# Two-operand VectorE operations in a four-layer mixer: the mean feature stays in PSUM, row sums move to GpSimd, the second batch is transposed by DMA, and the order of the work is written anew

## The chip, the cores and the metric

The kernel runs on one core of a Trainium2 chip: TensorE (PE, matmuls), VectorE (DVE), ScalarE (ACT), GpSimd (POOL) and SyncE (SP, which only issues DMAs here). The metric is the device time in microseconds (us) of one execution; a kernel is given by the median of its runs. All data is fp32. [...]

## The reference

Eight batches of 512 rows and 256 features pass through four layers, each added to its input `x` after a layer norm of it.

```python
x = x + attn_a(ln(x))            # Q, K = l2norm(x Wq), l2norm(x Wk); V = x Wv
                                 # Q * mean over rows of (K * V)
x = x + ffn(ln(x))               # "f": r * (relu(xk Wk)^2 Wv), r = sigmoid(xr Wr)
                                 # xr = mu_r x + (1-mu_r) x_prev, xk likewise; x_prev: the row before
x = x + attn_b(ln(x))            # 16 heads of 64: q, k, v with biases,
                                 # softmax over the queries (axis=2), output weights and bias
x = x + ffn(ln(x))               # "g", the same weights as "f"
```

## The kernel before, in words

**Stages and names.** In names, `b` is the batch, `h` one of two halves of 256 rows, `u` one of two blocks of 128 rows in a half. A batch passes through: `linear` and `queries` (layer one's K, V, Q, prefix `a`), `mean` and `front` (the mean feature and its product with Q), `front_ffn` (prefix `f`), `front_norm` (prefix `n`: the norm for the attention), then the attention, `project_out` or `project_out_fast` (tiles `m_y`), and `tail` (the second ffn, prefix `g`). The attention runs over `g` = 8 b + p, pairs of heads: `project_pairs` makes `qk` of two pairs with seven products in place of eight (`seven`, tiles `m_qk`, drained by ACT at L957 and DVE at L901, L911, L921, L965); `values_fast` does the same for `v` (tiles `m_v`). Then for each of four chunks `c` of 128 keys: `scores` (PE, L1258, tile `sc`), the maximum over the queries (DVE, L1263, `nm`), `exps` (ACT, L1274, `e`, with sums), `scale_v` (DVE reciprocal L1287, POOL product L1291, `vs`), `context` (PE, L1311, `cx`), drained at L1318 and L1319. Tiles that end in `True` belong to batch 1, and to the second ffn of batches 0 to 6; those in `False` to the other fronts and to `g7`.

**The order is written out by a planner.** The class `Order` takes generators ("chains") that yield steps: an engine, a cost in us, a time from which it may run. It keeps a clock for each engine and emits the instructions in the order in which it lets the steps run; the program fixes that order for every engine. Two pairs of heads form a period; `attend` writes their attention out, and `until` and `fill` put the other chains between, after due times in `PLAN` and a row of `CHOICES` for each period (a share of time, a slack, a seed for the ranks, and shifts of single chains). The planner also hands out five PSUM places: three of two banks (scores take them first) and two of one (context takes those). An engine runs its instructions strictly in the order written, so a late one holds all behind it.

**Norms.** `normed` takes the mean and variance (DVE, L377, L378, tiles `st`, `mv`); POOL then makes `shift` and `rstd` with two operations with constants (L395, L396; the early form has one, L383), a power (L397, L384) and a product (L398); ACT (L401) or, in the early form, DVE (L387) applies them. The result is turned either by PE (`normed_t`, L415, four transposes of 128 x 128 and a copy out of PSUM) or by a DMA (`normed_dma`: two POOL copies that set 16-bit halves apart, L428; a DMA transpose on SP's queue, L433; a POOL copy back, L437). Before the change batches 0 and 1 take PE at every norm of their front, the later ones the DMA.

**Time mixing.** `mixed_t` (from PSUM, L491, L501) and `mixed_dma` (from SBUF, L526, L532) form `xr` and `xk`; `first_column` fills the first row of a half from the last row of the half before (`edge`, L471).

**The mean feature.** `mean` multiplies a matrix of 1/512 with the products of K and V (L738), ACT copies the PSUM result to `gf` in SBUF (L741) and the bank is free; `front` then has DVE form `q * rn * gf` in four instructions a batch (L753), and adds it to `x` (L627; DVE for batches 0 and 1, and for the last tail, else POOL). `rows_of_output` ends with DVE adding the attention's result to `x` (L1199).

**Loads.** SP's queue issues x0, weights, x1, `aq`, `ak`, `av`, then `al` (written at L1352), x2 and x3. The biases are loaded from POOL's queue by `load_biases` (L331 to L335) within `mean` of batch 0. Batch 0's `v` are plain matmuls (`values`, L1024): eight blocks of two matmuls of 512 columns.

Of the kernel before, what the change touches and what calls it, by code (L numbers as in the profile page):

```python
# [8 lines left out]
F32 = mybir.dt.float32  # L9
# [29 lines left out]
    (3, 0, 38258, (9, 6)), (2, 0, 40677), (1, 0, 35919), (0, 0, 10543), (5, 2, 39456, (56, 6)),  # L39
    (4, 1, 34514), (2, -1, 72430), (6, 0, 70518), (1, 2, 57519), (4, 1, 11881), (0, 0, 0),  # L40
    (2, 0, 49737, (112, 6), (111, -24), (107, -24)), (-4, 1, 2083), (-3, -1, 8923),
    (-1, -1, 78359), (-3, 0, 30936), (-1, 1, 3181), (-1, 0, 25662, (161, 6)), (5, -1, 77260),
    (-2, 0, 42609), (-3, 0, 9127), (-2, 0, 32981), (2, -1, 46208), (-2, 0, 74670),
    (0, 1, 37804, (203, -6)), (3, 0, 36325),
    (3, 2, 41178, (216, 24), (219, -12), (217, 6), (240, 12)), (0, 0, 57144, (247, -24)),
    (5, 2, 47853), (4, 2, 81239), (-2, 2, 86574), (1, 0, 68043), (1, 0, 9189), (-4, 0, 55291),
# [12 lines left out]
    "v 0": (-1, 0), "v 1": (3, 0), "project": (-1, 0), "sums": (0, 0), "late sums": (5, 0),  # L59
# [34 lines left out]
class Order:  # L94
# [5 lines left out]
    def __init__(self):  # L100
        self.free = {"T": 0.0, "A": 0.0, "V": 0.0, "G": 0.0, "S": 0.0}
        self.chains, self.period, self.spent, self.count = [], -1, 0.0, 0
        self.open = -1
        self.marks = {None: 0.0}

        self.banks = [0.0] * (PAIRS + BANKS)
        self.current, self.at = None, 0.0
# [79 lines left out]
    def first(self, a):  # L187
        c = min(a, key=self.start)
        same = [d for d in a if d.on == c.on and self.start(d) <= self.start(c) + 0.4]
        return min(same, key=lambda d: (d.rank > -NP and d not in self.banks, d.rank + self.turn(d)))  # L190
# [5 lines left out]
    def turn(self, c):  # L196

        v, n = self.choice[2], c.number
        moved = sum(by for m, by in self.choice[3:] if m == n)
        if v == 0:  # L200
            return moved
        h = (n * 2654435761 + v * 40503 + v * n % 97 * 7919) & 0xFFFFFFFF
        h = ((h ^ h >> 13) * 1274126177) & 0xFFFFFFFF
        return ((h >> 8) % 1000 / 1000 - 0.5) * (24, 12, 6)[v % 3] + moved
# [49 lines left out]
def kernel(ctx: ExitStack, tc: tile.TileContext, a: dict, out: bass.AP):  # L254
# [73 lines left out]
    dvb = const.tile([P, 2, 2 * P], F32, tag="dvb", name="dvb")  # L328

    def load_biases():  # L330
        nc.gpsimd.dma_start(out=vb, in_=a["vb"].partition_broadcast(P))  # L331
        nc.gpsimd.dma_start(out=bias[:, 0, :], in_=a["qb"])
        nc.gpsimd.dma_start(out=bias[:, 1, :], in_=a["kb"])
        nc.gpsimd.dma_start(out=lb[:, 0, :], in_=a["lb"].partition_broadcast(P))
        nc.gpsimd.dma_start(out=lc, in_=a["lb"].rearrange("(k p) -> p k", p=P))  # L335
        order.place("G", 2.0, 0.0)
# [34 lines left out]
    def normed(src, name, s, h, ready, early=False):  # L371

        ready = yield "V", 1.2, ready
        mv = small.tile([P, 2, 2], F32, tag="mv", name=f"mv_{name}_{h}")
        for u in range(2):
            st = small.tile([P, 6], F32, tag="st", name=f"st_{name}_{h}_{u}")
            nc.vector.bn_stats(st, src[:, 2 * h + u, :])  # L377
            nc.vector.bn_aggr(mv[:, u, :], st)  # L378
        xn, rstd = tiles(s["xn"], h), small.tile([P, 2], F32, tag="rstd", name=f"rstd_{name}_{h}")
        if early:  # L380

            ready = yield "G", 1.05, ready
            nc.gpsimd.tensor_scalar(rstd, mv[:, :, 1], LN_EPS, 1.0, ALU.add, ALU.mult)  # L383
            nc.gpsimd.tensor_tensor(rstd, rstd, neg_half[:, :2], ALU.pow)  # L384
            ready = yield "V", 0.75, ready
            for u in range(2):
                nc.vector.tensor_scalar(  # L387
                    xn[:, u, :], src[:, 2 * h + u, :], mv[:, u, 0:1], rstd[:, u : u + 1],
                    ALU.subtract, ALU.mult,
                )  # L390
        else:

            shift = small.tile([P, 2], F32, tag="shift", name=f"shift_{name}_{h}")
            ready = yield "G", 1.4, ready
            nc.gpsimd.tensor_scalar(shift, mv[:, :, 0], -1.0, None, ALU.mult)  # L395
            nc.gpsimd.tensor_scalar(rstd, mv[:, :, 1], LN_EPS, 1.0, ALU.add, ALU.mult)  # L396
            nc.gpsimd.tensor_tensor(rstd, rstd, neg_half[:, :2], ALU.pow)  # L397
            nc.gpsimd.tensor_tensor(shift, shift, rstd, ALU.mult)  # L398
            ready = yield "A", 1.0, ready
            for u in range(2):  # L400
                nc.scalar.activation(  # L401
                    xn[:, u, :], src[:, 2 * h + u, :], AF.Identity,
                    bias=shift[:, u : u + 1], scale=rstd[:, u : u + 1],
                )
        return ready
# [60 lines left out]
    def first_column(prev, name, h, i):  # L466

        if h == 0:
            nc.vector.memset(prev[:, :, 0:1], 0.0)
        else:  # L470
            nc.vector.tensor_tensor(  # L471
                prev[:, :, 0:1], edge[name], omu[:, i, :].unsqueeze(2), ALU.mult
            )
# [256 lines left out]
    def mean(b, ready):  # L730

        if b == 0:
            nc.gpsimd.tensor_scalar(omu, mu, -1.0, 1.0, ALU.mult, ALU.add)
            order.place("G", 0.2, 0.0)
            load_biases()
        ready = yield "T", 0.43, ready
        ps = bank(f"gf_{b}")
        nc.tensor.matmul(ps[:, :D], lhsT=mean_s, rhs=means[b], start=True, stop=True)  # L738
        ready = yield "A", 0.3, ready
        gf = one.tile([P, D], F32, tag="gf", name=f"gf_{b}")  # L740
        nc.scalar.copy(gf, ps[:, :D])  # L741
        order.give()
        for h in range(2):
            order.add(front(b, h, gf, ready), *due_of("front", b))

    def front(b, h, gf, ready):
# [3 lines left out]
        ready = yield "V", 0.79, ready, -1, ("q", b, h)  # L750
        rn, qs = halves[b, h], tiles(s["r"], h)
        for u in range(2):
            nc.vector.scalar_tensor_tensor(  # L753
                qs[:, u, :], qs[:, u, :], rn[:, u : u + 1], gf, ALU.mult, ALU.mult
            )
# [3 lines left out]
    def front_ffn(b, h, ready):  # L759

        ready = yield from ffn(
            x[b], f"f{b}", buffers(b == 1), h, ready, adder(b), b >= 2, None
# [3 lines left out]
    def front_norm(b, h, ready):  # L766
# [9 lines left out]
        if b < 2:  # L776
# [10 lines left out]
        if not both(f"f{b}"):  # L787
            if b == 0:
                order.add(values(0, 0), "v 0")
                order.add(values(0, 1), "v 1")  # L790
# [183 lines left out]
    def values_fast(b, half):  # L974
# [5 lines left out]
        yield "G", 0.0, 0.0, -1, ("vs", NP * (b - 1) + 3 + 4 * half, 1)  # L980
# [33 lines left out]
    def values(b, half):  # L1014
# [3 lines left out]
        for t in range(NT):  # L1018
# [9 lines left out]
            issued("plain_v", 2 * NT, done)  # L1028
# [148 lines left out]
    def rows_of_output(b, h, ready):  # L1177
# [19 lines left out]
        ready = yield "V", 0.62, ready  # L1197
        xt = half_of(x[b], h)
        nc.vector.tensor_tensor(xt, s["xn"][:, h, :], xt, ALU.add)  # L1199
# [170 lines left out]
    order.add(sums_of_weights(av, "sums_v", split_values, "plain_v"), "late sums")  # L1370
# [88 lines left out]
```

## Time and profile before

| what | value | from |
|---|---|---|
| median of 3 runs | 1143.93 us (1142.75 to 1144.15) | the times |
| the profiled execution's own time | 1144.05 us | its run |
| its span, first to last instruction | 1142.3 us | the page |
| first matmul starts | 6.34 us | timeline |
| last matmul starts | 1136.86 us | trace |
| granted TensorE clock | 1.00 of full speed | view of the cores |
| moved by DMA | 33.10 MB, mean 29 GB/s | the page |
| DVE maximum of the scores (L1263) | 306.9 us in 256 instructions | groups |
| ACT exponentials (L1274) | 346.5 us in 512 instructions | groups |

A page has the busy time of each engine, the span in 40 slices, the DMA queues, the chain of work that ended last, and the costliest groups of instructions. A row of a group reads: line, engine, operation, output<-inputs, shapes, xcount | busy us, mean ns of one | the engine's idle time just before, and what ended most of it. A timeline's row has start, length, engine, line, operation, tiles, shapes, count, and in brackets the idle time before it with its releaser. In this trace an fp32 matmul has two records, a transpose one.

### The profile page before, as it was taken

To read this page: it belongs to the slowest core of one execution; us is meant where nothing else is said; L and a number is where in the kernel's file an instruction comes from. 1 tells how busy PE (TensorE), PEld (TensorE's weight loads), DVE (VectorE), ACT (ScalarE), POOL (GpSimd) and SP (SyncE) were. 2 spreads that over 40 slices of the span, in tenths; PEclk is the share of its full clock that TensorE was granted. 3 is DMA by queue.
4 is the path that set the end of the run, shared out by engine and by line. 5 is a ranking of instruction groups with operands and counts; after the bars stand their busy time and mean duration, and the time that the engine had idled before them with its cause. 6 is when DMAs were issued, how large, how long until landed. Compare 5 with 4: busy or idle time off the path is not lost.

```text
span 1142.3 us, 19417 instructions
## 1 busy us (share of the span) xinstructions
PE 1116.8 (98%) x6942; PEld 698.6 (61%) x6942; DVE 805.7 (71%) x1470; ACT 676.4 (59%) x1785; POOL 568.8 (50%) x883
## 2 busy tenths in 40 slices
PE   7999999999999999999999999999999999999998
PEld 4654556665756667565676656676565765656556
DVE  4877577678577785777857777668776677665755
ACT  4557665377455774556745676457755477554753
POOL 4475224554465544655546555465454754343321
PEclk9999999999999999999999999999999999999999
DMA  8001000110111100122011120121101110001101
GB/s 299 1 1 20 1 1 1 38 28 11 19 38 38 28 11 19 38 38 29 10 29 35 31 29 10 39 37 20 29 19 29 20 38 20 10 11 28 20 1 37
DMA packets 78640, 33.10 MB, mean 29 GB/s; under 512 B 68401, under 2 KB 77105, under 8 KB 78033
## 3 DMA queue, kind: packets, MB, share of 16 engines
q1 hardware_dynamic: 77360, 30.16, 11.8%
q8 instruction: 55, 0.90, 0.3%
q10 hardware_dynamic: 864, 1.05, 0.3%
q0 software_dynamic: 320, 0.67, 0.2%
q14 instruction: 41, 0.33, 0.1%
HBM read 10.89 MB, written 4.19 MB: 13 GB/s over the span
## 4 chain that ended last, share of the span: by engine, by line
PE 88%; DVE 6%; ACT 3%; issue 1%; POOL 1%; DMA 1%; DVEq 0%; POOLq 0%; ACTq 0%
PE sc L1258 19%; PE cx L1311 18%; PE m_qk L949 14%; PE m_v L985 8%; PE m_y L1129 7%; PE kv L681 5%; PE r_g L449 2%; PE o_f L449 2%; PE k_f L560 2%; PE r_f L449 2%; PE q L449 2%; PE m_k_g L600 2%; PE o_g L449 2%; ACT e L1274 2%; DVE xkFalse L753 1%; PE y L449 1%
## 5 line engine op out<-in xcount | busy, mean ns | idle before, releaser
L1274 ACT ACTIVATE e<-sc,nm 128x512 f32<-128x512 f32 x512 | 346.5, 691 | 149.3 <-DVE nm L1263 149.2
L1263 DVE TENSOR_REDUCE nm<-sc 128x2 f32<-128x1024 f32 x256 | 306.9, 1215 | 50.3 <-PE sc L1258 48.9
L1258 PE MATMUL sc<-qk 64*64 64x512 f32 x2048 | 274.0, 595 | 6.9 <-ACT e L1274 3.8
L1311 PE MATMUL cx<-e,vs 64*64 64x512 f32 x2048 | 273.2, 590 | 0.0
L1291 POOL TENSOR_TENSOR vs<-v,rs 128x256 f32<-128x256 f32 x128 | 82.9, 650 | 292.1 <-DVE rs L1287 280.7
L1311 PEld LDWEIGHTS cx<-e,vs 64*64 64x64 f32 x2048 | 92.0, 133 | 131.7 <-issue 104.9
L1258 PEld LDWEIGHTS sc<-qk 64*64 64x64 f32 x2048 | 78.5, 132 | 140.8 <-issue 70.4
L1274 ACT ACTIVATION_READ_ACCUMULATOR e<-sc,nm 128x1 f32 x512 | 106.4, 208 | 0.0
L957 ACT ACTIVATE qk<-m_qk,bias 128x256 f32<-128x256 f32 x124 | 52.0, 475 | 49.9 <-PE m_qk L949 42.4
L1319 DVE TENSOR_TENSOR ctx<-cx,ctx 128x512 f32<-128x512 f32 x64 | 44.2, 691 | 47.1 <-ACT ctx L1318 46.0
L965 DVE SCALAR_TENSOR_TENSOR qk<-m_qk,dbias,qk 128x256 f32<-128x256 f32 x124 | 54.2, 478 | 22.8 <-PE m_qk L949 21.9
L681 PE MATMUL kv<-wkv,xrFalse 128*128 128x512 f32 x112 | 54.0, 610 | 0.7 <-ACT xrFalse L668 0.7
L428 POOL COPY xrFalse<-xnFalse 128x512 uint16<-128x512 uint16 x72 | 41.7, 612 | 11.3 <-ACT xnFalse L401 11.3
L1318 ACT COPY ctx<-cx 128x512 f32<-128x512 f32 x64 | 37.6, 587 | 11.7 <-PE cx L1311 11.7
L437 POOL COPY xrFalse<-xkFalse 128x1024 uint16<-128x1024 uint16 x24 | 31.8, 1335 | 22.9 <-DMA xkFalse<-xrFalse 22.8
L949 PE MATMUL m_qk<-xts,aq 128*128 128x256 f32 x124 | 38.4, 392 | 4.7 <-DVE qk L965 4.5
L949 PE MATMUL m_qk<-xta,aq 128*128 128x256 f32 x124 | 39.9, 403 | 0.0
L1129 PE MATMUL m_y<-ctx,al 128*128 128x256 f32 x168 | 39.7, 379 | 0.0
L949 PE MATMUL m_qk<-xta,sums_q 128*128 128x256 f32 x124 | 37.1, 381 | 0.0
L949 PE MATMUL m_qk<-xta,ak 128*128 128x256 f32 x124 | 36.9, 379 | 0.0
L949 PE MATMUL m_qk<-xta,sums_k 128*128 128x256 f32 x124 | 36.9, 379 | 0.0
L949 PE MATMUL m_qk<-xts,ak 128*128 128x256 f32 x124 | 36.9, 379 | 0.0
(285 smaller groups left out, 2116.7 us busy)
## 6 DMA issues: line engine op xcount, KB each, us to landing
out<-x SPq DMA_DIRECT2D x16, 256.0 KB, 2.1
x<-in_x SPq DMA_DIRECT2D x6, 512.0 KB, 4.8
aq<-in_aq SPq DMA_DIRECT2D x1, 1024.0 KB, 8.2
ak<-in_ak SPq DMA_DIRECT2D x1, 1024.0 KB, 10.2
av<-in_av SPq DMA_DIRECT2D x1, 1024.0 KB, 12.2
al<-in_al SPq DMA_DIRECT2D x1, 1024.0 KB, 14.3
xkFalse<-xrFalse SPq DMA_TRANSPOSE x36, 3.1
x<-in_x ACTq DMA_DIRECT2D x4, 128.0 KB, 4.1
```

Source lines behind the costliest of these rows:

```text
L449: nc.tensor.matmul(ps[:, u * D : (u + 1) * D], lhsT=lhs[i][:, u * P : (u + 1) * P], rhs=rhs[i], start=(i == 0), stop=(i == n - 1),)
L681: nc.tensor.matmul(ps, lhsT=xt[:, kc, u * P : (u + 1) * P], rhs=wkv[:, kc, :], start=(kc == 0), stop=(kc == KC - 1),)
L949: nc.tensor.matmul(ps[:, w * HS : (w + 1) * HS], lhsT=lhs[w][n - 1], rhs=block_of_rows(b, n), start=start and w == 0, stop=True, skip_grou ...
L957: nc.scalar.activation(dst[:, w, :], ps[:, w, :], AF.Identity, bias=bias[:, w, p : p + 1])
L965: nc.vector.scalar_tensor_tensor(dst[:, w, :], ps[:, w, :], dbias[:, w, p // 2 : p // 2 + 1], part[:, w, :], ALU.add, ALU.add,)
L985: nc.tensor.matmul(ps[:, u * HS : (u + 1) * HS], lhsT=block_of_rows(b, n)[:, u * P : (u + 1) * P], rhs=rhs[n - 1], start=start and u == 0, ...
L1129: nc.tensor.matmul(ps, lhsT=lhs[n - 1][:, g, :], rhs=rhs[g][n - 1], start=first and g == 0, stop=True, skip_group_check=True,)
L1258: nc.tensor.matmul(ps[m * HD : (m + 1) * HD, j, :], lhsT=kt[hs, keys], rhs=qt[hs, :], start=True, stop=True,)
L1263: nc.vector.tensor_reduce(nm, ps, AX.X, ALU.max, negate=True)
L1274: nc.scalar.activation(e[:, j, :], ps[:, j, :], AF.Exp, bias=nm[:, j : j + 1], accum_out=sums[g, h][:, c % 2, j : j + 1],)
L1291: nc.gpsimd.tensor_tensor(vs, vh[b, p // 4][:, 2 * h : 2 * h + 2, cols].rearrange("p t (j d) -> p t j d", j=2), rs.unsqueeze(3).to_broadca ...
L1311: nc.tensor.matmul(cx[m][j * HD : (j + 1) * HD, :], lhsT=vsc[g, c // 2][ks, c % 2, j, :], rhs=es[g, c][ks, j, :], start=(c == 0), stop=(c ...
```

## The change

Seven edits go together:

1. `mean` no longer copies the mean feature to SBUF; DVE reads it in PSUM, and the bank is held until both halves of Q are multiplied.
2. `rows_of_output` adds rows on POOL in place of DVE.
3. `first_column` multiplies with `tensor_scalar`, one instruction for each of two feature blocks, in place of one `tensor_tensor`.
4. `normed` forms `rstd` and `shift` on DVE in place of POOL.
5. Batch 1's norms `f` and `n` are turned by DMA (and batch 1's `f` is mixed from SBUF); since `f1` no longer takes `mixed_t`, it no longer takes the early form of the norm.
6. Batch 0's second half of `v` takes seven products in place of eight.
7. The biases are loaded from SP's queue at the start; the planner gets another tie-break ("forks"), new costs for the moved steps and a new `CHOICES`, so every engine's order differs.

In the diff most of the rows of `CHOICES` are left out.

```diff
@@ -36,14 +36,23 @@
 
 
 CHOICES = (
-    (3, 0, 38258, (9, 6)), (2, 0, 40677), (1, 0, 35919), (0, 0, 10543), (5, 2, 39456, (56, 6)),
...
+    (0, 2, 3079, ((24, 1), (96, 3), (103, 1), (117, 1), (138, 1), (143, 1), (144, 1))),
...
-    "v 0": (-1, 0), "v 1": (3, 0), "project": (-1, 0), "sums": (0, 0), "late sums": (5, 0),
+    "v 0": (-1, 0), "v 1": (3, 0), "project": (-1, 0), "sums": (0, 0), "late sums": (5, 0), "sums v": (1, 0),
...
-        return min(same, key=lambda d: (d.rank > -NP and d not in self.banks, d.rank + self.turn(d)))
+        c = min(same, key=lambda d: (d.rank > -NP and d not in self.banks, d.rank + self.turn(d)))
+        forks = self.choice[3]
+        if self.period != self.last:
+            self.last, self.asked = self.period, 0
+        self.asked += 1
+        for at, other in forks:
+            if at == self.asked:
+                others = sorted((d for d in a if d is not c), key=self.start)
+                return ([c] + others)[min(other, len(others))]
+        return c
...
-    def load_biases():
-        nc.gpsimd.dma_start(out=vb, in_=a["vb"].partition_broadcast(P))
-        nc.gpsimd.dma_start(out=bias[:, 0, :], in_=a["qb"])
-        nc.gpsimd.dma_start(out=bias[:, 1, :], in_=a["kb"])
-        nc.gpsimd.dma_start(out=lb[:, 0, :], in_=a["lb"].partition_broadcast(P))
-        nc.gpsimd.dma_start(out=lc, in_=a["lb"].rearrange("(k p) -> p k", p=P))
-        order.place("G", 2.0, 0.0)
+    nc.sync.dma_start(out=vb, in_=a["vb"].partition_broadcast(P))
+    nc.sync.dma_start(out=bias[:, 0, :], in_=a["qb"])
+    nc.sync.dma_start(out=bias[:, 1, :], in_=a["kb"])
+    nc.sync.dma_start(out=lb[:, 0, :], in_=a["lb"].partition_broadcast(P))
+    nc.sync.dma_start(out=lc, in_=a["lb"].rearrange("(k p) -> p k", p=P))
+
...
-        ready = yield "V", 1.2, ready
+        ready = yield "V", 1.3 if early else 1.4, ready
...
         xn, rstd = tiles(s["xn"], h), small.tile([P, 2], F32, tag="rstd", name=f"rstd_{name}_{h}")
+        nc.vector.tensor_scalar(rstd, mv[:, :, 1], LN_EPS, None, ALU.add)
         if early:
 
-            ready = yield "G", 1.05, ready
-            nc.gpsimd.tensor_scalar(rstd, mv[:, :, 1], LN_EPS, 1.0, ALU.add, ALU.mult)
+            ready = yield "G", 0.75, ready
             nc.gpsimd.tensor_tensor(rstd, rstd, neg_half[:, :2], ALU.pow)
...
             shift = small.tile([P, 2], F32, tag="shift", name=f"shift_{name}_{h}")
-            ready = yield "G", 1.4, ready
-            nc.gpsimd.tensor_scalar(shift, mv[:, :, 0], -1.0, None, ALU.mult)
-            nc.gpsimd.tensor_scalar(rstd, mv[:, :, 1], LN_EPS, 1.0, ALU.add, ALU.mult)
+            nc.vector.tensor_scalar(shift, mv[:, :, 0], -1.0, None, ALU.mult)
+            ready = yield "G", 0.9, ready
             nc.gpsimd.tensor_tensor(rstd, rstd, neg_half[:, :2], ALU.pow)
             nc.gpsimd.tensor_tensor(shift, shift, rstd, ALU.mult)
             ready = yield "A", 1.0, ready
...
-            nc.vector.tensor_tensor(
-                prev[:, :, 0:1], edge[name], omu[:, i, :].unsqueeze(2), ALU.mult
-            )
+            for kc in range(KC):
+                nc.vector.tensor_scalar(
+                    prev[:, kc, 0:1], edge[name][:, kc, :], omu[:, i, kc : kc + 1], None, ALU.mult
+                )
...
             nc.gpsimd.tensor_scalar(omu, mu, -1.0, 1.0, ALU.mult, ALU.add)
             order.place("G", 0.2, 0.0)
-            load_biases()
         ready = yield "T", 0.43, ready
         ps = bank(f"gf_{b}")
         nc.tensor.matmul(ps[:, :D], lhsT=mean_s, rhs=means[b], start=True, stop=True)
-        ready = yield "A", 0.3, ready
-        gf = one.tile([P, D], F32, tag="gf", name=f"gf_{b}")
-        nc.scalar.copy(gf, ps[:, :D])
-        order.give()
         for h in range(2):
-            order.add(front(b, h, gf, ready), *due_of("front", b))
-
-    def front(b, h, gf, ready):
+            ready = yield "V", 0.79, ready, -1, ("q", b, h)
+            rn, qs = halves[b, h], tiles(buffers(b == 1)["r"], h)
+            for u in range(2):
+                nc.vector.scalar_tensor_tensor(
+                    qs[:, u, :], qs[:, u, :], rn[:, u : u + 1], ps[:, :D], ALU.mult, ALU.mult
+                )
+            if h == 1:
+                order.give()
+            order.add(front(b, h, ready), *due_of("front", b))
+
+    def front(b, h, ready):
 
 
         xb, s = x[b], buffers(b == 1)
-        ready = yield "V", 0.79, ready, -1, ("q", b, h)
-        rn, qs = halves[b, h], tiles(s["r"], h)
-        for u in range(2):
-            nc.vector.scalar_tensor_tensor(
-                qs[:, u, :], qs[:, u, :], rn[:, u : u + 1], gf, ALU.mult, ALU.mult
-            )
         ready = yield from add_to(xb, h, s["r"][:, h, :], ready, adder(b))
         order.add(front_ffn(b, h, ready), *due_of("ffn", b))
 
     def front_ffn(b, h, ready):
 
         ready = yield from ffn(
-            x[b], f"f{b}", buffers(b == 1), h, ready, adder(b), b >= 2, None
+            x[b], f"f{b}", buffers(b == 1), h, ready, adder(b), b >= 1, None
         )
         order.add(front_norm(b, h, ready), *due_of("norm", b))
 
@@ -773,7 +786,7 @@
                 xta[b] = two.tile([P, KC, S], F32, tag="xta", name=f"xta_{b}")
             return xta[b]
 
-        if b < 2:
+        if b < 1:
             ps, ready = yield from normed_t(xb, f"n{b}", s, h, ready, last)
             ready = yield "A", 0.5, ready
             nc.scalar.copy(of_half()[:, :, h * HS : (h + 1) * HS], ps)
@@ -787,7 +800,7 @@
         if not both(f"f{b}"):
             if b == 0:
                 order.add(values(0, 0), "v 0")
-                order.add(values(0, 1), "v 1")
+                order.add(values_fast(0, 1), "v 1")
         else:
             if b:
                 order.add(sums_of_rows(b, ready), "rows", NP * b)
@@ -977,7 +990,8 @@
         rhs = blocks_of_weights(av, blocks["sums_v"], split_values, half)
         if "sums_v" not in order.marks:
             yield "G", 0.0, 0.0, -1, "sums_v"
-        yield "G", 0.0, 0.0, -1, ("vs", NP * (b - 1) + 3 + 4 * half, 1)
+        if b:
+            yield "G", 0.0, 0.0, -1, ("vs", NP * (b - 1) + 3 + 4 * half, 1)
         v = vh[b, half] = one.tile([P, NT, 512], F32, tag=f"v{half}", name=f"v_{b}_{half}")
 
         def mul(ps, n, start):
@@ -1025,7 +1039,7 @@
                     ps, lhsT=xta[b][:, kc, t * P : (t + 1) * P], rhs=av[:, kc, cols],
                     start=(kc == 0), stop=(kc == KC - 1),
                 )
-            issued("plain_v", 2 * NT, done)
+            issued("plain_v", NT, done)
             ready = yield "V", 0.62, done
             nc.vector.tensor_tensor(vh[b, half][:, t, :], ps, vb[:, cols], ALU.add)
             order.give()
@@ -1194,9 +1208,9 @@
             y.rearrange("p (u d l) -> p l u d", l=2, u=2),
             turned.rearrange("p (l u d) -> p l u d", l=2, u=2),
         )
-        ready = yield "V", 0.62, ready
+        ready = yield "G", 1.3, ready
         xt = half_of(x[b], h)
-        nc.vector.tensor_tensor(xt, s["xn"][:, h, :], xt, ALU.add)
+        nc.gpsimd.tensor_tensor(xt, s["xn"][:, h, :], xt, ALU.add)
         order.add(tail(b, h, ready), "tail 6" if b == B - 2 else "tail", NP * b)
 
     def tail(b, h, ready):
@@ -1367,7 +1381,7 @@
         order.add(project(g), "project")
     order.add(sums_of_weights(aq, "sums_q", split_pairs, "plain_qk"), "sums")
     order.add(sums_of_weights(ak, "sums_k", split_pairs, "plain_qk"), "sums")
-    order.add(sums_of_weights(av, "sums_v", split_values, "plain_v"), "late sums")
+    order.add(sums_of_weights(av, "sums_v", split_values, "plain_v"), "sums v")
     order.add(sums_of_weights(fk, "sums_f", split_pairs, None), "late sums")
     order.add(sums_of_output(), "late sums")
     order.until(-1)
```

## The prediction, made before the changed kernel ran

> **What bounds the kernel.** First the page: busy times, and the chain of work that ended last.
>
> ```profile
> PE 1116.8 (98%) x6942; PEld 698.6 (61%) x6942; DVE 805.7 (71%) x1470; ACT 676.4 (59%) x1785; POOL 568.8 (50%) x883
> ...
> PE 88%; DVE 6%; ACT 3%; issue 1%; POOL 1%; DMA 1%; DVEq 0%; POOLq 0%; ACTq 0%
> ```
>
> PE sets the end; the others have 29% or more idle. So an edit is worth the PE work it takes away plus the PE stalls it ends; DVE or POOL time alone is worth nothing. Start to start, the timeline shows 0.43 us for an fp32 matmul of 256 columns (two records of 216 ns), 0.86 us for 512, 0.11 us for a transpose. I went through all successive starts for gaps: between the first and the last matmul 42 us are not matmul time. 20.4 us of these are 244 gaps of at most 0.13 us, mostly where the kind of matmul changes; I leave them. 3.2 us fall before 13 us, at the start. The other **18.4 us in 30 gaps** are what a better order can win.
>
> Second, the groups by shape: the same DVE instruction with different durations.
>
> ```profile
> L753 DVE SCALAR_TENSOR_TENSOR xkFalse<-xkFalse,rnq,gf 128x256 f32<-128x256 f32 x28 | 23.3, 876 | 3.4 <-ACT gf L741 3.3
> ...
> L471 DVE TENSOR_TENSOR prev_g<-edge_g,omu 128x2 f32<-128x2 f32 x14 | 6.8, 488 | 0.1
> ...
> L387 DVE TENSOR_SCALAR xnTrue<-x,mv_f,rstd_f 128x256 f32<-128x256 f32 x4 | 3.6, 934 | 0.0
> ...
> L471 DVE TENSOR_TENSOR prev_f<-edge_f,omu 128x2 f32<-128x2 f32 x12 | 2.1, 177 | 0.0
> ...
> L387 DVE TENSOR_SCALAR xnFalse<-x,mv_f,rstd_f 128x256 f32<-128x256 f32 x4 | 1.5, 408 | 0.2 <-POOL rstd_f L384 0.2
> ...
> L753 DVE SCALAR_TENSOR_TENSOR xkTrue<-xkTrue,rnq,gf 128x256 f32<-128x256 f32 x4 | 1.7, 470 | 0.0
> ...
> L1356 DVE TENSOR_SCALAR bias<-bias 128x8 f32<-128x8 f32 x1 | 0.7, 705 | 0.0
> ```
>
> The mean after the bar differs: 876 against 470, 488 against 177, 934 against 408. Third, the timeline around one of the long ones:
>
> ```profile
> 457.35 2.59 DVE L753 SCALAR_TENSOR_TENSOR xkFalse<-xkFalse,rnq,gf 128x256 f32<-128x256 f32 x2
> ...
> 458.20 1.46 POOL L627 TENSOR_TENSOR x<-x,xrTrue 128x512 f32<-128x512 f32 x1
> ...
> 459.86 3.47 DVE L1263 TENSOR_REDUCE nm<-sc 128x2 f32<-128x1024 f32 x3
> ...
> 461.11 0.69 ACT L1274 ACTIVATE e<-sc,nm 128x512 f32<-128x512 f32 x1 [6.18 <-DVE nm L1263]
> ...
> 462.61 0.66 PE L1258 MATMUL sc<-qk 64*64 64x512 f32 x4 [1.05 <-ACT e L1274]
> ```
>
> DVE's two instructions last until POOL's addition ends (459.66); the maxima behind them start late, so do the exponentials, and PE waits for a free score place. Gaps of this origin lie before `sc` at 323.27 (0.72 us), 462.61 (1.23), 602.45 (0.52), 741.78 (1.23) and 880.43 (0.53), each 4 to 7 us after a long L753, and at 532.83 (0.67) after a 1.26 us L471: **4.9 us**.
>
> **The change, part by part**, against this execution's own 1144.05 us.
>
> *PE work.* Batch 1's `f` and `n` lose 16 transposes: 16 x 0.11 = 1.7 us. Batch 0's second `v`: 8 matmuls x 0.86 = 6.9 become 14 x 0.43 = 6.0, 0.8 less with rounding. Sum **-2.6 us**, sure, since PE is full there.
>
> *Mean feature in PSUM (1), row additions on POOL (2).* L753 should take 470 ns: (876-470) x 28 = 11.4 us less DVE time, and 8 ACT copies (0.39 each) go. L1199 leaves DVE (10.9 us); POOL pays 14 x 1.3 = 18 us by L627's rows, 0.6 us more latency each, in a chain due 15 periods later. Of this PE sees the 4.9 us of gaps: **-4.9** (bounds -6 and -3). The bank's hold costs PE nothing in the order I read: the four multiplications follow the matmul on DVE, before or beside the next scores.
>
> *Norms (4) and edges (3).* 64 `rstd` and 56 `shift` operations at L471's clean 0.16 us are at most 19 us more on DVE, and 64 edges replace 32: 5 us more. POOL loses 54 x 0.22 + 64 x 0.19 = 24 us. DVE's net is some 5 us less; POOL's is near zero, with (2), batch 1's copies (8 x 0.61 + 4 x 1.34) and the biases' issues gone (3.0) too. [...] Removed waits: 11.4 + 4.6 (L471, `prev_g`) + 2.1 (L387) + 1.2 (L1199) = 19.3 us, which made 4.9 us of gaps: 0.25 us of gap for one of wait. Short waits did less (six L471 of 0.7 us each are followed by no gap). So between 0 and 12 x 0.25 = 3: **+1.5**.
>
> *Opening.* Gone: the gaps at 29.95 (0.63: `gf`'s copy on ACT, POOL's bias issues until 25.14), 43.04 (1.26: L501 stood behind other DVE work; the new order has it in front) and 45.35 (0.39): -2.3. New: `v_0_0_0` stands directly behind its transposes and must wait for ACT's copy (0.2 + 0.58); so does `v_0_0_2`; and the second half's transposes come 4.7 us after `o_f0_1`, whose chain (L578 0.69, addition 0.69, statistics 1.2, two scalars 0.2, power and product 0.9, L401 1.0, six handovers 0.1) takes 5.3: +0.8 +0.8 +0.6 = +2.2. Sum **0**.
>
> *SP's queue.* Five bias issues go before `al` (0.5 us each, hidden: `vb` is first read near 50 us). But `al`, x2 and x3, issued at 10 us before, now stand behind `f1`'s first transpose, near 50 us, and its second stands behind their 2 MB. `aq` to `al` landed 2 us apart, so 2 MB hold it 4 to 5 us. POOL's copy back (L437) then waits up to 3 us, with `sums_f`, `sums_q`, `vs_0_0`, `sums_k` behind it: 15 us of POOL before `m6_qk_2` needs them, which PE reaches some 23 us later. The slack of 7 us hides it: 0; if the transpose came 10 us late, PE would lose 3.
>
> *New order, middle.* Six gaps of 0.88 us (268.20, 407.04, 547.58, 686.21, 825.56, 964.20: PE waits for L965 behind an L532 pair) come from the order itself. Read in the new order, such a pair stands there four times: -1.8 at the old price; norms with their two scalars stand there elsewhere. I take **-1.0**. For places I can't follow: bounds -3 and +6, taken **+1.0**.
>
> *End.* The new order pulls the second ffn of batch 6 ahead of batch 7's. Between `tr_g7_0` and `k_g7_0` stand 2.15 us of matmuls; before, the way took 3.1 us (1118.44 to 1121.58) with DVE busier: **+0.7**. From `o_g7_1` on it is the same.
>
> Sum: -2.6 -4.9 +1.5 +0 -1.0 +1.0 +0.7 = -5.3, so 1138.75; this execution lies 0.12 above the median, so **1138.6 us**.
>
> **The rivals.**
> - *The waits only move* (slower). The small scalars stand before the maxima in DVE's queue. At 0.25 us of gap for one of wait, the gains of 2.6 + 4.9 + 1.0, less 1.7 for end and order, are eaten at 27 us of waits, and the kernel is slower by 2.3 us from 36 us, 0.2 us for each of the 184. At 0.35 us each: 64 x 0.25 = 16, so 1144.05 - 6.8 + 16 = 1153. For it: L1356. Against it: POOL is idle at most ends of norms, and POOL's next step then waits for this very DVE result.
> - *The gaps refill.* 18.4 us stay, at other places; only PE work goes, with the end's +0.7: 1144.05 - 2.6 + 0.7 = 1142. For it: every order written here left gaps. Against: the six L753 gaps have a cause that goes.
> - *The change does more.* Half of the 18.4 us goes, with no new waits: 1144.05 - 2.6 - 9.2 = 1132.
> - *It doesn't do what it says.* Batch 0's and 1's additions (L627) and L704 still read two SBUF operands; their rows show no long waits, so nothing changes.
>
> **How the numbers follow.** Forecast 0.60, its own range 1134 to 1143; waits move 0.16; refill 0.16; more 0.08. A measurement here tells about 0.2% (2.3 us) from no change: faster is below 1141.6. From the forecast 0.57, "more" 0.08, refill 0.05: faster 0.70; same 0.03 + 0.11 = 0.14; slower 0.16. The range, 1131 to 1148, takes in refill, most of "more", and the near part of the moved waits.
>
> **What would show it.** L753 near 470 ns with no POOL row ending beside it, and no gap before `sc` after it; the row addition on POOL at 1.3 us; `rstd` and `shift` near 0.16 us in the mean, the edges too (0.35 or more would be the slower rival); `tr_f`, `tr_n` without `xnTrue`; gaps before `v_0_0_0`, `v_0_0_2` and `k_g7_0` of 0.6 to 0.8 us; no POOL wait over 5 us for the second transpose of `f1`. A PE gap over 3 us anywhere would make the prediction wrong.

## The result: 1134.3 us, and the profile after

The changed kernel takes **1134.3 us** in the median of 4 runs (1133.06 to 1135.51), beside 1143.59 of the kernel before: ratio 0.9919, 95% interval 0.9902 to 0.9936, a gain of some 9 us (7.3 to 11.2) where 5.3 were forecast. The time is inside the range; the gain was under-estimated. One execution of e5 below, its profiled one, took 4979.55 us with the matmuls several times as long (a record of `sc` 2246 ns in the mean, 594 in the changed kernel), and is left out of that run's ratio.

The page after has the same reading: PE sets the end. DVE has 7 us more to do (812.7 us against 805.7), where the prediction had some 5 us less; most of the difference is the waits of `rstd` and `shift` below (10.7 us).

```profile
span 1133.7 us, 19490 instructions
...
PE 1112.3 (98%) x6938; PEld 687.1 (61%) x6938; DVE 812.7 (72%) x1607; ACT 675.8 (60%) x1779; POOL 562.4 (50%) x789
```

Of the gain, 2.6 us are matmul work; the rest has to be looked for between the matmuls. I went through the successive starts again, in both traces with the same cost for each kind (429.3 ns for 512 columns, 215.8 for 256, 109.2 for a transpose, 858.6 for eight records of the 64-row kind; by these costs the gaps before come to 45.4 us, where the prediction counted 42). From the first to the last matmul:

| us | before | after | difference |
|---|---|---|---|
| first to last matmul | 1130.52 | 1121.99 | -8.5 |
| matmul work | 1085.16 | 1082.59 | **-2.6** |
| gaps | 45.36 | 39.40 | **-6.0** |
| of these, before `sc` after a held L753 or L471 (six, and an echo of 0.22 some 6.5 us after each) | 6.2 | 0 | -6.2 |
| before `m_qk`, behind a mixing pair | 5.3 | 1.3 | -4.0 |
| before `sc` at 100, 153, 1063 (after: 405, 1055), with what led up to them | 4.5 | 2.1 | -2.4 |
| before `sc`, `cx` and `m_qk` after a held `rstd` or `shift` (473, 658, 660, 934, 937) | 0 | 4.0 | +4.0 |
| before `cx`, for POOL's `vs` (968, 1042) | 0 | 1.8 | +1.8 |
| opening, 14 to 60 | 2.5 | 2.5 | 0.0 |
| end, before `tr_g` and `k_g` of batch 7 | 0 | 0.6 | +0.6 |
| before 14 us, at four other places, and 0.13 to 0.25 each elsewhere | 6.3 | 8.0 | +1.7 |
| up to 0.13 us each | 20.6 | 19.2 | -1.4 |

Single values are good to 0.1 us or so; the last two rows are what is left. The 8.5 us are the difference of the two profiled executions (1144.05 and 1135.51 us); the medians differ by 9.3.

The groups by shape show what became of the waits (bar: busy, mean ns):

```profile
L758 DVE SCALAR_TENSOR_TENSOR xkFalse<-xkFalse,rnq,gf 128x256 f32<-128x256 f32 x28 | 11.7, 474 | 2.8 <-POOL rnq L673 2.8
...
L396 DVE TENSOR_SCALAR rstd_f<-mv_f 128x2 f32<-128x2 f32 x16 | 7.3, 459 | 0.6
L487 DVE TENSOR_SCALAR prev_f<-edge_f,omu 128x1 f32<-128x1 f32 x28 | 6.1, 219 | 0.9 <-ACT prev_f L542 0.2 <-ACT edge_f L536 0.2
```

L758 is the L753 of before, at 474 ns where it took 876. The timeline shows that it no longer waits for POOL (start, length): four of them in a row, with one addition of POOL inside and the next beginning before they end.

```profile
451.35 1.65 DVE L758 SCALAR_TENSOR_TENSOR xkFalse<-xkFalse,rnq,gf 128x256 f32<-128x256 f32 x4
451.51 1.28 POOL L643 TENSOR_TENSOR x<-x,xrTrue 128x512 f32<-128x512 f32 x1 [0.42 <-DVE xrTrue L594]
```

In its place `rstd` is late. Of the 120 `rstd` and `shift`, 22 take over 0.27 us, 10.7 us of waits in all, and each of the 22 ends 22 to 28 ns after an instruction of POOL does. Here a POOL copy of 16-bit halves holds it for 1.14 us; what is queued behind it on DVE, the drain of `m_qk` (L934) and the edge, is late too, and PE has to wait twice, 0.46 us before `sc` and 1.18 before `cx` by the starts:

```profile
653.41 2.57 POOL L452 COPY xrTrue<-xkTrue 128x1024 uint16<-128x1024 uint16 x2
...
654.70 1.31 DVE L396 TENSOR_SCALAR rstd_n<-mv_n 128x2 f32<-128x2 f32 x1
...
656.90 0.69 DVE L934 TENSOR_TENSOR qk<-m_qk,qk 128x512 f32<-128x512 f32 x1
...
657.65 1.09 PE L1272 MATMUL sc<-qk 64*64 64x512 f32 x8 [0.30 <-DVE qk L934]
...
659.69 1.09 PE L1325 MATMUL cx<-e,vs 64*64 64x512 f32 x8 [0.95 <-DVE prev_g L484]
```

### The profile page after: what moved, and what is told of

Same layout as the page of the kernel before. It is cut to its first block, busy times and chain, and to the rows that moved or that the text cites. A ratio compares the mean times of both kernels' runs of the same rounds, so it can differ in the third digit from the quotient of the medians.

```text
span 1133.7 us, 19490 instructions
## 1 busy us (share of the span) xinstructions
PE 1112.3 (98%) x6938; PEld 687.1 (61%) x6938; DVE 812.7 (72%) x1607; ACT 675.8 (60%) x1779; POOL 562.4 (50%) x789
## 3 DMA queue, kind: packets, MB, share of 16 engines
q10 hardware_dynamic: 864, 1.05, 0.3%
## 5 line engine op out<-in xcount | busy, mean ns | idle before, releaser
L1272 PE MATMUL sc<-qk 64*64 64x512 f32 x2048 | 264.1, 594 | 2.4 <-DVE qk L934 1.5
L1325 PE MATMUL cx<-e,vs 64*64 64x512 f32 x2048 | 262.5, 590 | 3.7 <-DVE prev_g L484 1.9
L1305 POOL TENSOR_TENSOR vs<-v,rs 128x256 f32<-128x256 f32 x128 | 78.7, 615 | 268.5 <-DVE rs L1301 250.2
L1325 PEld LDWEIGHTS cx<-e,vs 64*64 64x64 f32 x2048 | 82.8, 133 | 142.7 <-issue 114.4
L1272 PEld LDWEIGHTS sc<-qk 64*64 64x64 f32 x2048 | 74.2, 132 | 138.4 <-issue 81.2
L703 ACT COPY av<-kv 128x256 f32<-128x256 f32 x32 | 12.0, 374 | 59.4 <-PE kv L697 58.1
L643 POOL TENSOR_TENSOR x<-x,xkFalse 128x512 f32<-128x512 f32 x24 | 30.3, 1274 | 15.4 <-DVE xkFalse L594 10.4
```

What stands on the lines that cost most here:

```text
L1272: nc.tensor.matmul(ps[m * HD : (m + 1) * HD, j, :], lhsT=kt[hs, keys], rhs=qt[hs, :], start=True, stop=True,)
L1305: nc.gpsimd.tensor_tensor(vs, vh[b, p // 4][:, 2 * h : 2 * h + 2, cols].rearrange("p t (j d) -> p t j d", j=2), rs.unsqueeze(3).to_broadca ...
L1325: nc.tensor.matmul(cx[m][j * HD : (j + 1) * HD, :], lhsT=vsc[g, c // 2][ks, c % 2, j, :], rhs=es[g, c][ks, j, :], start=(c == 0), stop=(c ...
```

## The experiments

Apart from the matmul work, the prediction ascribes the gain to the operands (edits 1 to 4) and nearly nothing to the new order. The rival after the result: the order brought it. Most runs keep the changed kernel's order, every instruction at its place, and alter only an engine or an operand. Times are medians in us, ratios against runs of the kernel before on the same chip.

| run | median | ratio, 95% interval | first to last matmul | gaps |
|---|---|---|---|---|
| before | 1143.59 | 1 | 1130.5 | 45.4 |
| changed | 1134.3 | 0.9919 (0.9902 to 0.9936) | 1122.0 | 39.4 |
| e1, edits 1 to 4 taken back | 1153.96 | 1.0089 (1.0075 to 1.0102) | 1142.9 | 60.3 |
| e2, edit 1 taken back | 1145.46 | 1.0011 (1.0003 to 1.0020) | 1132.9 | 50.3 |
| e3, edit 4 taken back | 1135.38 | 0.9923 (0.9909 to 0.9936) | 1123.1 | 40.5 |
| e4, one-element `rstd`, `shift` | 1130.53 | 0.9886 (0.9871 to 0.9901) | 1116.7 | 34.2 |
| e5, e11, `gf` copied in PSUM | 1135.19 | 0.9922 (0.9908 to 0.9936) | 1120.8 | 38.3 |
| e6, edit 2 taken back | 1141.71 | 0.9980 (0.9973 to 0.9988) | 1129.5 | 46.9 |
| e7, edit 3 taken back | 1132.02 | 0.9900 (0.9885 to 0.9915) | 1118.2 | 35.6 |
| e8, before with edits 2, 3, 4 | 1147.44 | 1.0029 (1.0018 to 1.0041) | 1133.3 | 48.1 |
| e9, e4 and e7 together | **1127.68** | 0.9867 (0.9852 to 0.9882) | 1114.1 | 31.5 |
| e12, e4 with edges on ACT | 1135.76 | 0.9934 (0.9922 to 0.9947) | 1122.5 | 39.9 |
| e10, edits 1 to 4, another order | 1229.17 | 1.0749 (1.0731 to 1.0766) | 1217.0 | |

### e1: the new order with the old operands

```diff
-                nc.vector.scalar_tensor_tensor(qs[:, u, :], qs[:, u, :], rn[:, u : u + 1], ps[:, :D], ...)
+                nc.vector.scalar_tensor_tensor(qs[:, u, :], qs[:, u, :], rn[:, u : u + 1], gf, ...)
-        nc.gpsimd.tensor_tensor(xt, s["xn"][:, h, :], xt, ALU.add)
+        nc.vector.tensor_tensor(xt, s["xn"][:, h, :], xt, ALU.add)
```

and likewise the edges as one `tensor_tensor`, `rstd` and `shift` on POOL, as in the kernel before.

> The changed kernel in its own written order (every engine's instructions at their places), with edits 1 to 4 taken back in the instructions alone: the mean feature is copied to SBUF by ACT (eight copies more, no place planned for them) and read there, the rows are added by DVE, the edges are one tensor_tensor, rstd and shift are made by POOL. Left of the change: the new order, batch 1's norms by DMA, the cheaper v, the loads. Theory 'operands': the waits for POOL were worth most of the gaps, so the additions of POOL hold the DVE again at the five or six mean-feature places, 4 to 7 us of gaps come back, and the time is 1138 to 1142 us. Rival 'order': the gaps went because the new order is better and the operands hardly matter: 1133 to 1136 us.

Measured: 1153.96, 19.7 us more than the changed kernel, where the "operands" theory expected 4 to 8. With the old operands the new order loses 10 us to the old order, although it has 2.6 us less PE work. The order alone brings nothing; this one gains only with the durations for which it was written. e1 keeps edits 5 to 7, which no run takes back singly.

### e2, e5 and e11: edit 1 alone, and its two halves

```diff
         nc.tensor.matmul(ps[:, :D], lhsT=mean_s, rhs=means[b], start=True, stop=True)
+        gf = one.tile([P, D], F32, tag="gf", name=f"gs_{b}")
+        nc.scalar.copy(gf, ps[:, :D])
```

with `gf` in place of `ps[:, :D]` in the product (e2); for e5 the copy is `nc.scalar.copy(ps[:, :D], ps[:, :D])`, and DVE reads `ps` as in the changed kernel.

> The changed kernel with edit 1 alone taken back in place: one ACT copy of the mean feature for each batch (0.39 us each), DVE reads the copy in SBUF. Theory 'operands': in the changed kernel 18 of the 28 L758 run at 474 ns inside POOL additions L643 of 1.28 us; read in SBUF, the second pair of each batch 3 to 7 waits for the addition's end again, so their mean is 800 to 900 ns, and gaps of 0.5 to 1.2 us come before sc some 4 to 7 us later: +3.5 to +5 us, 1138 to 1139.5 us. Rival 'order': the scores stand at places where DVE has time to spare: L758 waits, but 1134 to 1135.5 us.

> The changed kernel with the eight ACT copies of the mean feature put back, but from its PSUM bank onto itself: DVE waits for ACT as in the run with the copy in SBUF, at the same places of the same order, and still reads PSUM. It parts the two halves of that run's loss of 11 us. Theory 'operand': the loss came from L760's waits for POOL's additions (mean 864 against 474 ns, 11 us of DVE time, six PE gaps of 0.5 to 1.7 us before sc): here L758 is at 474 ns and the time is 1134 to 1137 us. Rival 'handover': ACT's late copies (5.1 us of DVE idle time against 2.8) made the gaps: L758 at 474 ns, but 1140 to 1146 us.

Measured: e2 1145.46, 11 us more, far over the 5 expected; e5 1135.19. e11 is the kernel of e5 once more, for its trace:

> The run with the mean feature's copy back onto its own bank once more, for a trace: L759 at 474 ns in the mean (864 with the copy in SBUF) although DVE waits for ACT's copy in both, no gaps over 1 us before sc near 321, 462, 740 and 880, and a span of 1133 to 1136 us.

It gave 1134.3 us. First the group in e2, then that in e11:

```profile
L760 DVE SCALAR_TENSOR_TENSOR xkFalse<-xkFalse,rnq,gs 128x256 f32<-128x256 f32 x28 | 22.7, 864 | 5.1 <-ACT gs L755 5.1
```

```profile
L759 DVE SCALAR_TENSOR_TENSOR xkFalse<-xkFalse,rnq,gf 128x256 f32<-128x256 f32 x28 | 11.7, 475 | 5.0 <-ACT gf L754 5.0
```

Both wait the same 5 us for ACT. Only the one that reads SBUF takes twice as long, and only it is slower: the handover costs nothing that can be measured, the operand's place 10 to 11 us. The timeline of e2 around one place shows how:

```profile
455.24 1.26 POOL L643 TENSOR_TENSOR x<-x,xrTrue 128x512 f32<-128x512 f32 x1 [0.42 <-DVE xrTrue L594]
455.37 3.62 DVE L760 SCALAR_TENSOR_TENSOR xkFalse<-xkFalse,rnq,gs 128x256 f32<-128x256 f32 x4 [0.20 <-ACT gs L755]
...
457.33 1.38 POOL L643 TENSOR_TENSOR x<-x,xkFalse 128x512 f32<-128x512 f32 x1 [0.82 <-DVE xkFalse L760]
...
458.91 3.47 DVE L1279 TENSOR_REDUCE nm<-sc 128x2 f32<-128x1024 f32 x3
...
461.66 1.09 PE L1274 MATMUL sc<-qk 64*64 64x512 f32 x8 [1.48 <-ACT e L1290]
```

The four products last 3.62 us in place of 1.65: the first waits for one addition, the last for the next, which the first two products have released. The maxima start that much later, and PE has a gap of 1.66 us before `sc`. Five gaps of 1.55 to 1.67 us and one of 0.53, with five echoes of 0.22 behind them, make 9.8 us, out of 10.9 us of waits (28 x 390 ns).

### e6: edit 2 alone

```diff
-        nc.gpsimd.tensor_tensor(xt, s["xn"][:, h, :], xt, ALU.add)
+        nc.vector.tensor_tensor(xt, s["xn"][:, h, :], xt, ALU.add)
```

> The changed kernel with edit 2 alone taken back in place: the 14 additions of rows are DVE's again. Theory: DVE gets 14.7 us more (1053 ns each, as in the run with all four edits taken back, where a clean one would be some 0.62), at places planned for POOL; the gap at 1041.7 (0.7 us, a row addition on POOL ahead of vs) goes, but the maxima behind the additions come late: +2 to +5 us, 1136 to 1139 us. Rival 'as priced in the prediction': PE sees nothing of it: 1133 to 1135.5 us.

Measured: 1141.71, more than either expected. Of the 14 additions nine take 0.68 us; five begin beside POOL's copy of the other half (L1207), last up to 1.72 and wait for 3.8 us together. The maxima follow directly behind them: most of the new gap time lies behind the five, but a clean addition at 774.75 too has a gap of 0.70 us behind it. The largest gap of the run, 2.94 us before `sc` at 1046.5, follows from one of them through the maximum and the exponential:

```profile
1042.09 1.71 DVE L1213 TENSOR_TENSOR x<-xnTrue,x 128x512 f32<-128x512 f32 x1 [2.24 <-POOL xnTrue L1207]
...
1043.72 1.21 DVE L1277 TENSOR_REDUCE nm<-sc 128x2 f32<-128x1024 f32 x1
...
1046.47 1.09 PE L1272 MATMUL sc<-qk 64*64 64x512 f32 x8 [2.76 <-ACT e L1288]
```

### e3, e4: the scalars of the norm

```diff
-        nc.vector.tensor_scalar(rstd, mv[:, :, 1], LN_EPS, None, ALU.add)
+        for u in range(2):
+            nc.vector.tensor_scalar(rstd[:, u : u + 1], mv[:, u, 1:2], LN_EPS, None, ALU.add)
```

for e4, `shift` likewise; for e3 both go back to POOL as in the kernel before.

> The changed kernel with edit 4 alone taken back in place: rstd and shift are formed by POOL again, at the front of POOL's part of the norm. Theory: the DVE's two rstd_n waits of 1.31 us and the locked pair near 470 us made the PE gaps at 657.7 and 659.7 (1.6 us), 934.5 and 936.6 (1.6 us) and 472.6 (0.7 us); they go, and POOL's 24 us more are hidden: -2.5 to -4 us, 1130 to 1132 us. Rival: what DVE saves POOL loses in the chains of the norms (0.2 to 0.4 us later each, POOL's copies behind them): the gaps go to other places, 1133 to 1137 us.

> The changed kernel with every rstd and shift made in two instructions of one element a partition in place of one of two elements: 120 DVE instructions more. Theory 'one element is exempt': the 64 edges of one element never waited for POOL (mean 221 ns, 203 at the least), while 22 of the 120 rstd and shift of two elements did, for 10.7 us. Then rstd and shift have no wait over 0.1 us, DVE gains 10.7 us of waits and loses 120 x 0.06 to 0.16 us, the gaps near 472, 658 and 935 go: 1130 to 1132 us. Rival 'luck of the places': the edges merely fell where POOL was idle; the first of each two waits as before, and with 7 to 19 us more DVE time: 1134 to 1138 us.

Measured: e3 1135.38, not to be told from the changed kernel, and so within its rival's range; e4 1130.53, as its theory had it. In e4 no one-element instruction is held:

```profile
L397 DVE TENSOR_SCALAR rstd_n<-mv_n 128x1 f32<-128x1 f32 x32 | 4.3, 137 | 0.0
```

At the place shown above, the two take 0.27 us in all inside the same copy of POOL:

```profile
652.23 2.58 POOL L454 COPY xrTrue<-xkTrue 128x1024 uint16<-128x1024 uint16 x2
...
653.41 0.27 DVE L397 TENSOR_SCALAR rstd_n<-mv_n 128x1 f32<-128x1 f32 x2
```

and the gap near 473 goes, those near 658 and 935 shrink from 1.6 us to 0.5 each. So the waits of the two-element scalars did make these gaps.

The gap near 968 goes too, but the traces put it down to a DMA. In the changed kernel POOL's copies stand behind a DMA transpose, and the `vs` that `cx` needs behind the copies:

```profile
962.25 2.60 POOL L452 COPY xta<-xkFalse 128x1024 uint16<-128x1024 uint16 x2 [4.48 <-DMA xkFalse<-xrFalse]
...
967.91 1.09 PE L1325 MATMUL cx<-e,vs 64*64 64x512 f32 x8 [0.91 <-POOL vs L1305]
```

This transpose landed 4.4 us after its issue. It took 4.3 to 4.8 us in e1, e2, e3, e6, e11 and e12, and all of them have the gap (1.0 to 1.9 us); it took 3.05 in e4, e7 and e9, and none of them has it. Why it lands at two times stays open; some 1.1 us of what the traces of e4, e7 and e9 gain are this gap.

But e3, which takes away the same waits as e4, gains nothing: there the gaps are before `sc` and `cx` at 491, 628, 630 and 769 (0.8 to 1.05 us). In e3 the edges stand behind POOL's late copies: 

```profile
L488 DVE TENSOR_SCALAR prev_f<-edge_f,omu 128x1 f32<-128x1 f32 x28 | 6.1, 219 | 4.9 <-ACT edge_f L537 3.0 <-ACT prev_f L543 1.2
```

DVE is idle 4.9 us before them, 0.9 in the changed kernel. POOL's 25 us more (587.9 against 562.4) come back, at 626 for one, as a chain POOL, ACT, DVE, PE: the wait has changed engines.

### e7, e9, e12: the edges

```diff
-            for kc in range(KC):
-                nc.vector.tensor_scalar(prev[:, kc, 0:1], edge[name][:, kc, :], omu[:, i, kc : kc + 1], None, ALU.mult)
+            nc.vector.tensor_tensor(prev[:, :, 0:1], edge[name], omu[:, i, :].unsqueeze(2), ALU.mult)
```

> The changed kernel with edit 3 alone taken back in place: each edge is one tensor_tensor of two elements in place of two tensor_scalar of one. Theory: the pairs wait for POOL here and there (318 ns in the mean in the run with all four taken back, 0.16 without a wait: 4.4 us of waits), but there are 28 instructions fewer of 219 ns, so DVE's sum falls by some 3 us, and what counts is where the long ones stand: 1133 to 1136.5 us. Rival: waits in front of the mixing pairs cost what the mean feature's cost (0.9 us of gap for one of wait): 1137 to 1139 us.

> The changed kernel with both edits that shortened it: rstd and shift in instructions of one element, and each edge again one tensor_tensor of two. Alone they gave 1130.5 and 1132.0 us against 1134.3. The gaps that each of them closes are partly the same (472.6 and 967.9, together 1.8 us), so not the whole 6.1 us is to be had: theory 1129 to 1131 us, with the one long edge near 520 us (1.28 us behind an addition) still making its gap of 0.6 us. Rival 'edges cost the same either way once the scalars don't wait': 1130.5 to 1132 us.

In e12, with e4's scalars, the same loop is `nc.scalar.activation(prev[:, kc, 0:1], edge[name][:, kc, :], AF.Identity, scale=omu[:, i, kc : kc + 1])`.

> The kernel with one-element rstd and shift, and the 64 edge products on ACT in place of DVE (scale in place of tensor_scalar, no place planned for them): DVE loses 64 x 0.22 = 14 us, ACT gets 64 x 0.2 = 13 us, the mixing pair behind them waits as long as before. It asks what edit 3's price was: theory 'DVE time in front of the mixing pair and the maxima': 1127.5 to 1130 us, since the pairs lose no DVE time to edges and ACT has 40% idle. Rival 'it is the chain, whichever engine does it, and ACT's exponentials come late': 1131 to 1135 us.

Measured: e7 1132.02, below the 1133 to 1136.5 expected; its interval overlaps that of the changed kernel, but its trace has 3.8 us less from first to last matmul, of which 1.1 are the gap at 968. e9 1127.68, below the 1129 to 1131 expected: 6.6 us less than the changed kernel, where the gains of e4 and e7 add up to 6.1. The wait of the edge near 520 us that e7 had (1.28 us) did not come in e9, where its edge fell beside no addition. e12 is worse than e4 by 5 us, nearest to its rival (1131 to 1135): ACT does the edges behind four activations of the same step, DVE waits for both, and PE for DVE, 2.18 us before `m_qk` at 263.9:

```profile
259.75 1.92 ACT L544 ACTIVATE prev_g<-xrTrue,omu 128x255 f32<-128x255 f32 x4
261.60 0.54 ACT L489 ACTIVATE prev_g<-edge_g,omu 128x1 f32<-128x1 f32 x2
...
262.23 0.87 DVE L550 SCALAR_TENSOR_TENSOR xkTrue<-xrTrue,mu,prev_g 128x256 f32<-128x256 f32 x2 [1.59 <-POOL shift_n L415]
```

(The releaser named was done at 261.76; the edges of ACT ended at 262.14.)

### e8, e10: the edits in other orders

e8 is the kernel before with edits 2, 3 and 4 at the instructions' old places, e10 the kernel before with edits 1 to 4, where the held bank makes the planner write another order from the old `CHOICES`.

> The kernel before in its own written order, with edits 2, 3 and 4 in place: row additions on POOL, edges as two tensor_scalar of one element, rstd and shift of two elements on DVE; the mean feature stays in SBUF (in place it would deadlock, since the bank is given on before DVE has read it). The other side of the square: the same edits in an order not written for them. Theory: the four L753 gaps of 0.5 to 1.2 us stay, the gap of 0.67 us after the 1.26 us edge goes, the new two-element scalars wait some 10 us and make 3 to 9 us of new gaps: 1145 to 1152 us. Rival 'the edits are good in any order': 1139 to 1143 us.

> The kernel before with edits 1 to 4, its planner and the numbers of its CHOICES left as they were: because the mean feature's bank is now held, the planner writes another order, about as far from the one before as the changed kernel's is (of PE's 1701 instructions 955 stand in common stretches, against 919), and one that nobody selected. Edits 5 to 7 are left out (+2.6 us of PE work). Theory 'an order has to be chosen for its durations': as with the old operands in the new order (61 us of gaps against 39 to 45 in the two selected pairs), 1150 to 1165 us. Rival 'the operands bring the gain, in nearly any order': 1136 to 1142 us.

Measured: e8 1147.44, within its range; e10 1229.17, far above both of its ranges. In e8 the loss has another reason than the one expected. None of its 118 `rstd` and `shift` was held, 160 ns in the mean: at these places POOL was never inside an instruction.

```profile
L396 DVE TENSOR_SCALAR rstd_n<-mv_n 128x2 f32<-128x2 f32 x16 | 2.6, 162 | 0.0
```

It loses all the same: the two scalars stand ahead of a drain of `m_qk`, so that each of the six gaps of 0.88 us grows to 1.02; gaps of 0.84 us before `tr_n` at 47 and of 0.78 before `sc` at 396 are new, and L754 stays at 877 ns. In e10, PE waits 14.3 us in 12 places for the drains of one line alone (L920), of which the one at the longest of them (4.1 us, before `sc` at 760) stands behind three mixing pairs in DVE's queue. Not all of e10's loss is waiting. In nine stretches of 51 us together its granted clock was 0.50 (0.979 in the mean), and a record of 256 columns took 427 ns there in place of 216; by the matmuls that start in them I estimate 21 us. With all four operand edits the other 65 us remain: an order that nobody chose for these durations cost far more time than the edits bring.

## Why the prediction was right, and where its sum was not

The forecast's mechanism held: L753's waits were the cause of gaps, its new form has no waits, and the six gaps are gone. The size, 9.3 us against 5.3 (8.5 in the two traces), comes from terms that were off in both directions and in part cancelled: that part of the agreement is luck.

- *PE work -2.6*: it is -2.57.
- *Mean feature -4.9*: right as a count of what goes, except that 0.22 us after each of the six gaps belong to them (1.3 more). The ratio of 0.25 us of gap for one of wait was the wrong measure for this place: e2 shows 9.8 for 10.9, or 0.9. What a wait costs depends on what is queued behind it: here maxima, with PE waiting for their scores.
- *Row additions: no gain on their own*. e6: 7.4 us in this order. I had counted the waits of L1199 (1.2 us) and put down the DVE time as worth nothing. In this order the additions on DVE would wait 3.8 us and stand in front of maxima; the runs do not part what the waits cost from what the DVE time costs.
- *New scalars +1.5 (0 to 3)*: **outside its own bounds**. The 12 us of waits in its sum were my estimate from the trace before: at 13 of the 64 ends of the second L378 POOL was busy, for 5.9 us more in all, and I doubled that for `shift`. No run shows 12; the trace after shows waits of 10.7 us, which made 4.0 us of gaps: the size of the waits was nearly right, the 0.25 us of gap for one of wait was not. e4, which only takes them away, gains 3.8. The edges, which I had counted among the instructions at risk, never waited (219 ns inside a POOL instruction, 215 outside). But two of them take some 0.45 us where a `tensor_tensor` takes 0.16 without a wait, and taking them back gains 2.3 us (e7) and, beside e4, 2.9 (e9), each with overlapping intervals. That they cost this because they stand in front of a mixing pair is argued, not tested.
- *Opening 0*: the gaps before `v` of 0.84 and 0.84 us came (predicted 0.8 and 0.8), `tr_n` made 0.8; 0.0 in all.
- *SP's queue 0*: right for the two transposes of `f1`, for which POOL waits less than 1.5 us. But POOL's longest wait for a DMA, 4.48 us at 962, stands before the gap of 1.12 us at 968; no term held such a wait.
- *Middle: -1.0 and +1.0*: the first was **mis-sized by 3**, the largest error of the sum. Of the places where a pair stands between two drains of `m_qk`, I priced four at the old 0.88 us. Only that at 263 made a gap (1.31 us). At the others PE has other work: eight matmuls of `r_g`, 1.7 us, beside the pair.

```profile
539.90 0.48 DVE L548 SCALAR_TENSOR_TENSOR xrTrue<-xrTrue,mu,prev_g 128x256 f32<-128x256 f32 x1
...
540.44 1.89 PE L464 MATMUL r_g<-fr,xrTrue 128*128 128x256 f32 x8
...
540.90 0.87 DVE L978 SCALAR_TENSOR_TENSOR qk<-m_qk,dbias,qk 128x256 f32<-128x256 f32 x2
```

  The places that I could not follow were taken at +1.0 and came to -0.3: -2.4 and +1.8 by the table, +1.7 and -1.4 in its small ones.
- *End +0.7*: 0.37 and 0.26 us, 0.63.

Of the rivals, "refill" is excluded by the measured interval (1142 would be a ratio of 0.998). "More", 1132, is near in time, but not for its reason, since new waits did come. "The waits move" is right that new waits come and make gaps, and wrong about the weight: it needed 27 us of waits, and 10.7 came.

One thing the sum could not say: here the parts gain nothing by themselves. The new order with the old operands costs 10 us more than the kernel before, three of the four operand edits in the old order 3 to 4 us more, and all together 9 us less. Taken back singly in the new order, edits 1, 2, 3 and 4 cost 11, 7, -2 and 1 us.

## What to carry to other kernels

Price a wait by what is queued behind it, not by one ratio for the kernel: a microsecond of wait on VectorE was worth 0.9 us of TensorE in front of a maximum (e2), and a mixing pair cost nothing where TensorE had eight other matmuls (1.7 us of `r_g`, changed kernel). A product of 256 elements that began inside a GpSimd instruction took 1115 ns in the mean with both inputs in SBUF (e2) and 474 with one of them in PSUM (changed kernel): where GpSimd is busy beside VectorE, try that move for large instructions with two inputs. Small `tensor_scalar` work from SBUF to SBUF paid one element at a time (e4, 1130.53 us against 1134.3); the edges, most of them into PSUM, did not (e7, which takes them back, 1132.02). After a change of operands choose the order again, and measure neither without the other.

## What the runs showed of the hardware

The prediction had not foreseen that one-element `rstd` and `shift` are not held (e4, 137 and 144 ns in the mean). VectorE instructions by whether they begin inside a GpSimd instruction, counted from the starts and lengths in the trace of the run that the row names (mean ns, count):

| operation, operands | inside | outside |
|---|---|---|
| `tensor_scalar`, 2 elements, SBUF to SBUF (L396, changed) | 458 (29) | 170 (35) |
| `tensor_scalar`, 1 element, SBUF to SBUF (L397, e4) | 137 (58), at most 155 | 137 (70) |
| `tensor_scalar`, 1 element, SBUF to PSUM (L487, changed; 8 of the 64 to SBUF) | 219 (37) | 215 (27) |
| `tensor_tensor`, 2 elements, two SBUF inputs (L486, e7) | 408 (15) | 159 (17) |
| `scalar_tensor_tensor`, 256, two SBUF inputs (L760, e2) | 1115 (17) | 475 (15) |
| the same, one input in PSUM (L758, changed) | 474 (23) | 473 (9) |
| mixing pair, `prev` in PSUM (L548, changed) | 478 (74) | 478 (38) |

The means inside take in instructions that begin just before POOL's ends. In e4, 73 of the one-element `rstd` and `shift` begin over 0.2 us before the end of a large GpSimd instruction, and none takes over 155 ns. Not every GpSimd instruction holds two elements: 15 that begin over 0.2 us before the end of a GpSimd operation of two elements a partition (L412, L673; 0.7 us) were not held in the changed kernel (159 to 170 ns). Why stays open.

Inside a GpSimd instruction, `tensor_scalar` from SBUF to SBUF took 137 ns in the mean with one element (e4) and 458 with two (changed); what makes them differ no trace shows.
